# An RWKV-6 block on one core: where the first norm's statistics are computed

## The chip, the cores and the metric

The kernel runs on one core of one Trainium2 chip. The core has a matrix engine (TensorE, PE in the profile, with its weight loads shown apart as PEld), three engines for elementwise work (VectorE or DVE, ScalarE or ACT, GpSimd or POOL), and queues from which transfers are started (here those of SyncE, called SP, and of ScalarE). Each engine works through its own list of instructions strictly in order; an instruction that waits holds up everything behind it on its engine. The metric is the device time of one execution in microseconds (us).

## The reference

The input x has 32 sequences of 128 tokens with 512 channels, in float32. For each sequence the block does:

- a first layer norm over the 512 channels, and a token shift (the difference of each token to the one before it);
- five mixed inputs, each the normed x plus the shift times (a constant + a low-rank tanh product);
- from these a decay `w` by two exponentials, and the products `r`, `k`, `v` and a gate `g`, each a 512x512 matrix product;
- a recurrence over the 128 tokens with a 16x16 state for each of 32 heads, its output normed per head, times the gate, times `Wo`, added to x;
- a second layer norm and a second shift, a squared-ReLU feed-forward with a sigmoid factor, added to x.

The part that the change touches is the first line of this:

```python
m = jnp.mean(x, axis=-1, keepdims=True)
v = jnp.mean((x - m) ** 2, axis=-1, keepdims=True)
return (x - m) * jax.lax.rsqrt(v + EPS) * w + b
```

## The kernel before

The 32 sequences are worked in eight groups of four (`GB` = 4, `NG` = 8); a sequence of a group is called a block b here, with 128 tokens in the partitions and 512 channels in a row. Each group passes through streams, written as Python generators: `front_mix` (load x, first norm, shift, mixed inputs), `front_proj` (decay, k, r, v, sent by DMA to a layout with one head in each partition), `front_gate`, `prep` (what the recurrence needs besides: products of r and k, called the bonus, and decays of pairs of tokens), the recurrence in 34 units of a group (`rec_act`, `rec_state`, `rec_pool`, `rec_dve`, `rec_pe`, `rec_out`), and `back` (head norm, gate, `Wo`, second norm, feed-forward). The last group's `back` is cut in two halves, "last1" and "last2".

The order of the work is not written by hand. While the kernel is built, a planner (`Plan`, lines 73 to 179) asks every stream for its next operation, computes from its own price list when each could start, and among those that could start within `EPSILON` of the earliest takes the one with the lowest due value. The due values run, for each stream, between the two numbers of `DUE` (line 49), in units of groups. So the planner's choice fixes the order of instructions on each engine, and the chip keeps that order whatever the real times are. Buffers are part of it: an operation that needs a new tile of a kind (`alloc`) can only be taken when one of that kind is free. There are four `blk` tiles (512 columns, used to evict products on their way to DMA, for the gate, and in the bonus), two `stats`, two `mv`, two `x`, three `mx`, one `ev`, and four `ps` banks for TensorE's results.

The first norm is in `layernorm_T` (line 326), called by `front_mix` with `sums` equal to None (line 458). Its statistics are lines 333 to 342: for each of the four blocks one `bn_stats` (L339) and one `bn_aggr` (L340) on DVE, which give mean and variance in `mv`. Then, for the whole group, DVE computes variance + eps (L357), POOL raises it to the power -0.5 (L359), DVE makes -mean times that (L361), and ACT applies both to each block (L368; in the first group DVE takes every second block, L365). The normed blocks are transposed by PE (L394), and evicted by ACT and DVE.

The second norm, called by `back` with `sums` given, goes another way: the sums come for free with the addition of the residual (L884, with an accumulator), DVE turns them into minus the mean (L347), and ACT squares x minus the mean of each block with an accumulator (L354), its main output going to an `ev` tile that is overwritten later.

In the recurrence each unit needs on POOL a product (L730) and a sum of pairs (L734), on ACT two copies (L705, L716), on DVE a scan (L752) and a product (L754), and on PE eight small transposing matmuls (L787). The bonus on DVE is L660 to L680.

Of the kernel before, what the change touches and what calls it, by code (L numbers as in the profile page):

```python
# [10 lines left out]
AF = mybir.ActivationFunctionType  # L11
ALU = mybir.AluOpType
# [3 lines left out]
B, L, E = 32, 128, 512  # L16
# [19 lines left out]
PE, DVE, ACT, POOL, SP = range(5)  # L36
# [6 lines left out]
LANDING = 2.0  # L43
HOP = (0.2, 0.05, 0.05, 0.04, 0.08)
ON_POOL = (2, 3, 4)
EPSILON = 0.039


DUE = {"rec": (0.171, 0.811), "mix": (-4.351, -2.486), "proj": (-6.56, 7.24), "gate": (0.525, 0.545), "prep": (-4.001, 1.375), "back": (-0.209, 3.178), "last1": (-27.722, 1.84), "last2": (7.448, 22.404)}


class Buf:
# [20 lines left out]
class Plan:  # L73
# [103 lines left out]
    def pick(self, best):  # L177
        t0 = min(t for t, _ in best)
        return min((x for x in best if x[0] <= t0 + EPSILON), key=lambda x: x[1][3] + x[1][4] * x[1][2])


@with_exitstack
def rwkv6_block(ctx: ExitStack, tc: tile.TileContext, x, prev, s0, vecs, u, maa_w1, maa_w2,
# [11 lines left out]
    nc = tc.nc  # L195
# [76 lines left out]
    def col(v, e):  # L272
        return vec[:, v, e : e + 1]

    def bt(ap):
        return ap.rearrange("p (b t) -> p b t", t=L)
# [45 lines left out]
    def part(us, bs):  # L322

        return us if len(bs) == GB else us * len(bs) / GB + 0.03

    def layernorm_T(g, src, sums, vw, vb, which, use, take, need=None, bs=range(GB)):

        b0, nb_ = bs[0], len(bs)
        bsl, cols = slice(b0, b0 + nb_), slice(b0 * L, (b0 + nb_) * L)
        if sums is None:
            xh = src
            stats, mv = yield Op(DVE, 0.88, r=[(src, b0)], w=[(0, b0), (1, b0)], alloc=["stats", "mv"])
            for b in bs:
                if b != b0:
                    yield Op(DVE, 0.88, r=[(src, b)], w=[(stats, b), (mv, b)])
                nc.vector.bn_stats(stats[:, b, :], src[:, b, :])  # L339
                nc.vector.bn_aggr(mv[:, b, :], stats[:, b, :])  # L340
            stats.open = False
            mean, var, scale = mv[:, bsl, 0], mv[:, bsl, 1], 1.0
        else:
            mv = sums
            yield Op(DVE, 0.16, r=[(mv, b) for b in bs], w=[(mv, "m")])
            mean, var, scale = mv[:, bsl, 0], mv[:, bsl, 1], 1.0 / E
            nc.vector.tensor_scalar(mean, mean, -1.0 / E, None, ALU.mult)  # L347
            xh = None
            for b in bs:
                if xh is None:  # L350
                    (xh,) = yield Op(ACT, 0.83, r=[(src, b), (mv, "m")], w=[(0, b), (mv, ("v", b))], alloc=["ev"])
                else:
                    yield Op(ACT, 0.83, r=[(src, b), (mv, "m")], w=[(xh, b), (mv, ("v", b))])
                nc.scalar.activation(xh[:, b, :], src[:, b, :], AF.Square, bias=mv[:, b, 0:1],  # L354
                                     accum_out=mv[:, b, 1:2])
        (rstd,) = yield Op(DVE, 0.16, r=[(mv, None)], w=[(0, None)], alloc=["rstd"], port=True)
        nc.vector.tensor_scalar(rstd[:, bsl], var, scale, EPS, ALU.mult, ALU.add)  # L357
        yield Op(POOL, 1.1, r=[(rstd, None)], w=[(rstd, None)], port=True)
        nc.gpsimd.tensor_tensor(rstd[:, bsl], rstd[:, bsl], mhalf[:, bsl], ALU.pow)  # L359
        (nb,) = yield Op(DVE, 0.16, r=[(mv, None), (rstd, None)], w=[(0, None)], alloc=["nb"], port=True, end=[mv])  # L360
        nc.vector.scalar_tensor_tensor(nb[:, bsl], mean, -1.0 if sums is None else 1.0, rstd[:, bsl], ALU.mult, ALU.mult)  # L361
        for b in bs:
            if g == 0 and sums is None and b % 2:
                yield Op(DVE, 0.5, r=[(src, b), (nb, None), (rstd, None)], w=[(xh, b)], port=True)
                nc.vector.tensor_scalar(xh[:, b, :], src[:, b, :], rstd[:, b : b + 1], nb[:, b : b + 1], ALU.mult, ALU.add)  # L365
                continue
            yield Op(ACT, 0.8, r=[(src, b), (nb, None), (rstd, None)], w=[(xh, b)])
            nc.scalar.activation(xh[:, b, :], src[:, b, :], AF.Identity, bias=nb[:, b : b + 1],  # L368
                                 scale=rstd[:, b : b + 1])
        rstd.open = nb.open = False  # L370
        (xnT,) = yield Op(ACT, 0.25, w=[(0, "p")], alloc=["xnT"], need=need)
        nc.scalar.copy(xnT[:, :, 0].rearrange("p (e b) -> p e b", b=GB)[:, :, bsl],
                       pv[:, 1 - which, :, g * GB + b0 : g * GB + b0 + nb_])
        late = []

        def evict(e, pt):
            if g == 0 and sums is None:

                yield Op(DVE, 0.69, r=[(pt, None)], w=[(xnT, e)])
                nc.vector.tensor_scalar(xnT[:, e * GB + b0 : e * GB + b0 + nb_, 1 : L + 1], bt(pt[:, cols]),  # L380
                                        col(vw, e), col(vb, e), ALU.mult, ALU.add)
            else:
                yield Op(ACT, part(0.78, bs), r=[(pt, None)], w=[(xnT, e)])
                nc.scalar.activation(xnT[:, e * GB + b0 : e * GB + b0 + nb_, 1 : L + 1], bt(pt[:, cols]), AF.Identity,
                                     bias=col(vb, e), scale=col(vw, e))
            yield from use(xnT, e, pt, tiles)

        for e in range(NE):
            if e == 0:
                pt, *tiles = yield Op(PE, 0.11 * nb_, r=[(xh, None)], w=[(0, None)], alloc=["ps", *take])  # L390
            else:
                (pt,) = yield Op(PE, 0.11 * nb_, r=[(xh, None)], w=[(0, None)], alloc=["ps"])
            for b in bs:
                nc.tensor.transpose(pt[:, b * L : (b + 1) * L], xh[:, b, e * P : (e + 1) * P], ident)  # L394
            late.append((e, pt))
            if len(late) > 1:
                yield from evict(*late.pop(0))
        xh.open = False
        yield from evict(*late.pop(0))
        return (xnT, *tiles)  # L400
# [38 lines left out]
    def front_mix(g, d):  # L439
# [8 lines left out]
        def use(xnT, e, pt, tiles):  # L448
# [7 lines left out]
            nc.vector.scalar_tensor_tensor(xin[:, e, :], sx[:, e, :], col(V_MAAX, e), pt.t, ALU.mult, ALU.add)  # L456

        xnT, sx, xin = yield from layernorm_T(g, xt, None, V_LN1W, V_LN1B, 0, use, ("sx", "mx"), need)
        d["xin"] = True
        if g == 0:  # L460
# [349 lines left out]
    def back(g, d, bs=range(GB), W=None):  # L810
# [90 lines left out]
        def receptance(xnT):  # L901
# [10 lines left out]
            return xr  # L912

        xnT, xk = yield from layernorm_T(g, x1, sums, V_LN2W, V_LN2B, 1, use, ("mx",), need, bs)
        fkt = yield from get("fk", fk)
        frt = yield from get("fr", fr)
# [56 lines left out]
    for gen, n in ((rec_dve, 2), (rec_pool, 3), (rec_act, 1), (rec_state, 1), (rec_pe, 2), (rec_out, 0.1)):  # L973
        v0, v1 = DUE["rec"]
        plan.add(gen(range(NG)), v0, NG - 1 + v1, n * NU * NG)
    for g in range(NG):
        for gen, name, n in ((front_mix, "mix", 40), (front_proj, "proj", 72), (front_gate, "gate", 17),
                             (prep, "prep", 40), (back, "back", 140)):
            v0, v1 = DUE[name]
            if name != "back" or g < NG - 1:  # L980
# [4 lines left out]
    for bs, name in (((0, 1), "last1"), ((2, 3), "last2")):  # L985
        v0, v1 = DUE[name]
        plan.add(back(NG - 1, data[-1], bs, W), NG - 1 + v0, NG - 1 + v1, 130)
# [38 lines left out]
```

## Time and profile before

| | |
|---|---|
| median of 3 runs | 1524.67 us (1521.03 to 1527.92) |
| the profiled execution, own time | 1523.82 us |
| its span, first to last instruction | 1522.0 us |
| mean granted TensorE clock | 0.963 |
| PE busy, share of the span | 1407.3 us, 92% |
| DVE busy | 1264.1 us, 83% |
| POOL busy | 1036.0 us, 68% |
| ACT busy | 652.7 us, 43% |
| first norm's statistics on DVE (L339, L340), 32 blocks | 27.2 us busy |

A line such as "L339 DVE BATCH_NORM_STATS2 stats<-x" is a group of instructions of line 339 of the kernel, on DVE, that write the tile `stats` and read `x`. In the timeline, the columns are the start, the length (from the first to the end of the last of xN instructions), engine, line and operation; in square brackets is the time that the engine sat idle before it, and whose result ended that. In the table by stretches of time, each engine's busy time stands with its number of instructions in brackets, then the granted TensorE clock, the share of the DMA engines and GB/s. Successive instructions of one engine overlap a little at their ends, so their sum can exceed the time that they take in a row.

### The profile page before, as it was taken

Reading aid. Unit: us, or ns where it says so; the run is one execution under the profiler, and the core shown is the slowest. Engines: PE = TensorE matmul, PEld = TensorE weight load, DVE = VectorE, ACT = ScalarE, POOL = GpSimd, SP = SyncE. Lnnn points to the kernel's source line nnn. Section 1 sums busy time; section 2 is a strip of 40 time slices with the busy share of each in tenths; the row PEclk is TensorE's granted clock in tenths of the full one; section 3 lists DMA queues with packets and bytes.
Section 4 is the critical chain, followed back from the end, with each engine's and each line's share of the span. In section 5 each row is a group of like instructions: output and inputs, shape, how many; then the busy total and the mean of one; then the engine's idle time right before and its main releaser. Section 6 shows DMA issues by size and latency. Waiting matters only on the chain.

```text
span 1522.0 us, 16610 instructions
## 1 busy us (share of the span) xinstructions
PE 1407.3 (92%) x5344; PEld 746.5 (49%) x5344; DVE 1264.1 (83%) x1614; ACT 652.7 (43%) x1271; POOL 1036.0 (68%) x642
## 2 busy tenths in 40 slices
PE   5897988889999999999999999999999999689778
PEld 2343454445554555445544555455544555455444
DVE  6539789888998899889988899899988898878732
ACT  3333243324743356423743366423843363344252
POOL 3225884877586959687786959687786959679500
PEclk9897899899999999999999999999999999889989
DMA  6130330424304531244304521244304421400220
GB/s 225 56 87 14 118 103 15 142 82 138 118 24 139 168 102 43 80 143 135 117 31 133 184 86 42 90 143 131 111 32 140 150 98 35 159 28 29 95 71 28
DMA packets 127879, 147.04 MB, mean 97 GB/s; under 512 B 8368, under 2 KB 77616, under 8 KB 126768
## 3 DMA queue, kind: packets, MB, share of 16 engines
q1 hardware_dynamic: 91312, 127.59, 25.4%
q10 hardware_dynamic: 36480, 18.39, 4.2%
q8 instruction: 42, 0.69, 0.2%
q14 instruction: 45, 0.37, 0.1%
HBM read 94.57 MB, written 17.83 MB: 74 GB/s over the span
## 4 chain that ended last, share of the span: by engine, by line
PE 51%; DVE 21%; POOL 18%; issue 5%; ACT 3%; DMA 2%; SPq 0%; POOLq 0%; DVEq 0%; ACTq 0%
PE ps L408 18%; POOL am L730 10%; PE acc L787 8%; PE ps L965 6%; POOL a L734 6%; PE ps L949 6%; PE ps L427 5%; DVE sc L752 4%; DVE rm L754 3%; PE ps L875 2%; PE ps L414 2%; PE ps L465 2%; DVE rk L668 1%; DVE ps L660 1%; POOL mx L488 1%
## 5 line engine op out<-in xcount | busy, mean ns | idle before, releaser
L730 POOL TENSOR_TENSOR am<-v,k 128x1024 f32<-128x1024 f32 x256 | 609.0, 2379 | 34.2 <-DMA r<-blk 15.6
L408 PE MATMUL ps<-mx,wt 128*128 128x512 f32 (+1 forms) x1312 | 585.0, 593 | 17.8 <-DVE mx L456 6.6
L734 POOL TENSOR_TENSOR a<-am 128x504 f32<-128x504 f32 x256 | 286.5, 1119 | 209.4 <-DVE sc L752 183.2
L408 PEld LDWEIGHTS ps<-mx,wt 128*128 128x128 f32 x1312 | 243.8, 194 | 287.4 <-issue 261.9
L752 DVE TENSOR_TENSOR_SCAN sc<-sc,a 128x512 f32<-128x512 f32 x256 | 313.4, 1224 | 35.4 <-POOL a L734 32.3
L754 DVE TENSOR_TENSOR rm<-sc,r 128x1024 f32<-128x1024 f32 x256 | 312.8, 1222 | 32.3 <-PE acc L787 17.1
L787 PE MATMUL acc<-by_head,rm 128*128 128x128 f32 x2176 | 291.5, 284 | 39.1 <-DVE rm L754 37.0
L787 PEld LDWEIGHTS acc<-by_head,rm 128*128 128x128 f32 x2176 | 254.0, 146 | 135.8 <-DVE rm L754 53.8
L705 ACT COPY sc<-w 128x512 f32<-128x512 f32 x256 | 151.2, 591 | 250.6 <-DVE rm L754 225.7
L488 POOL TENSOR_TENSOR mx<-mx,xnT 128x512 f32<-128x512 f32 x94 | 111.6, 1198 | 72.9 <-DVE mx L486 68.7
L716 ACT COPY a<-st 128x8 f32<-128x8 f32 x256 | 51.4, 203 | 153.4 <-DVE sc L752 131.9
L949 PE MATMUL ps<-wt,mx 128*128 128x512 f32 x256 | 115.7, 594 | 0.1
L875 PE MATMUL ps<-wt,mx 128*128 128x512 f32 x256 | 113.3, 600 | 0.2 <-DVE rk L668 0.2
L965 PE MATMUL ps<-wt,ev 128*128 128x512 f32 x224 | 103.2, 604 | 2.7 <-DVE mx L493 2.7
L562 ACT COPY blk<-ps 128x512 f32<-128x512 f32 x96 | 56.0, 583 | 103.8 <-PE ps L408 94.8
L359 POOL TENSOR_TENSOR rstd<-rstd,mhalf 128x4 f32<-128x4 f32 (+1 forms) x17 | 20.2, 1191 | 116.7 <-DVE rstd L357 116.7
L486 DVE SCALAR_TENSOR_TENSOR mx<-ps,vec,sx 128x512 f32<-128x512 f32 x94 | 69.0, 743 | 25.3 <-PE ps L427 25.1
L427 PE MATMUL ps<-tha,w2p 64*128 64x512 f32 x256 | 82.2, 674 | 3.4 <-DVE mx L493 3.4
L875 PEld LDWEIGHTS ps<-wt,mx 128*128 128x128 f32 x256 | 49.1, 194 | 60.9 <-issue 56.4
L491 DVE SCALAR_TENSOR_TENSOR ps<-ps,vec,sx 128x512 f32<-128x512 f32 x66 | 49.6, 752 | 31.7 <-PE ps L427 31.3
L949 PEld LDWEIGHTS ps<-wt,mx 128*128 128x128 f32 x256 | 46.4, 190 | 51.1 <-issue 46.9
L965 PEld LDWEIGHTS ps<-wt,ev 128*128 128x128 f32 x224 | 41.1, 193 | 45.8 <-issue 40.2
(110 smaller groups left out, 1331.4 us busy)
## 6 DMA issues: line engine op xcount, KB each, us to landing
x<-in_x SPq DMA_DIRECT2D x13, 1024.0 KB
wt<-in_wk SPq DMA_DIRECT2D x8, 1024.0 KB
wt<-in_wr SPq DMA_DIRECT2D x8, 1024.0 KB
wt<-in_wg SPq DMA_DIRECT2D x8, 1024.0 KB
dgate<-blk SPq DMA_DIRECT2D x32, 256.0 KB
wt<-in_wo SPq DMA_DIRECT2D x8, 1024.0 KB
wt<-in_fk SPq DMA_DIRECT2D x8, 1024.0 KB
wt<-in_fr SPq DMA_DIRECT2D x8, 1024.0 KB
```

The lines of the kernel that those rows point to most:

```text
L408: nc.tensor.matmul(p, lhsT=w[:, c, e * P : (e + 1) * P], rhs=xin[:, c, cols], start=(c == 0), stop=(c == NE - 1))
L427: nc.tensor.matmul(p.t, lhsT=w[h, :], rhs=t[h, :], start=True, stop=True)
L488: nc.gpsimd.tensor_tensor(bt(x5[:, f, :]), bt(x5[:, f, :]), row(xnT, f, 1), ALU.add)
L705: nc.scalar.copy(sc.t, d["w01"][:, q : q + 1, :].to_broadcast([P, DH, T2]))
L730: nc.gpsimd.tensor_tensor(am.t, v[:, ds, :], k[:, q : q + 1, :].to_broadcast([P, DH, L]), ALU.mult)
L734: nc.gpsimd.tensor_tensor(a[:, :, 1:T2], am2[:, :, 0 : T2 - 1, 0], am2[:, :, 0 : T2 - 1, 1], ALU.add)
L752: nc.vector.tensor_tensor_scan(scf, scf, a.t.rearrange("p d n -> p (d n)"), 0.0, ALU.mult, ALU.add)
L754: nc.vector.tensor_tensor(pair(rm.t), sc.t.unsqueeze(3).to_broadcast([P, DH, T2, 2]), r2[:, q : q + 1, :, :].to_broadcast([P, DH, T2, 2]), ...
L787: nc.tensor.matmul(acc[:, i, :], lhsT=rm[:, i, :], rhs=by_head, is_transpose=True, start=(q == 0 and i % 4 == 0), stop=(q == S), skip_grou ...
L875: nc.tensor.matmul(p.t, lhsT=att[:, c, b * L : (b + 1) * L], rhs=wot[:, c, :], start=(c == 0), stop=(c == NE - 1))
L949: nc.tensor.matmul(p.t, lhsT=xr[:, c, b * L : (b + 1) * L], rhs=frt[:, c, :], start=(c == 0), stop=(c == NE - 1))
L965: nc.tensor.matmul(p2.t, lhsT=kv[:, c, b * L : (b + 1) * L], rhs=fvt[:, c, :], start=(c == 0), stop=(c == NE - 1))
```

## The change

For all groups but the first, the statistics of the first norm move to ACT. For each block ACT runs over x once with `Identity` and an accumulator (the sum), DVE turns the four sums into minus the mean, and ACT runs over x a second time with `Square`, minus the mean as bias, and an accumulator (the sum of squared differences). The main outputs of the eight passes go to one `blk` tile that nobody reads. The operation after it divides by 512 as the second norm's does, and since the mean is now stored with its sign turned, L361's factor changes. The first group keeps `bn_stats`. The planner's price for each pass is 0.9 us. `EPSILON` and all the due values differ too, so the order of instructions is planned anew for the whole kernel.

```diff
-EPSILON = 0.039
-DUE = {"rec": (0.171, 0.811), "mix": (-4.351, -2.486), "proj": (-6.56, 7.24), "gate": (0.525, 0.545), "prep": (-4.001, 1.375), "back": (-0.209, 3.178), "last1": (-27.722, 1.84), "last2": (7.448, 22.404)}
+EPSILON = 0.0784
+DUE = {"rec": (0.026, 0.93), "mix": (-3.979, -2.846), "proj": (-9.769, 14.248), "gate": (-1.553, 1.011), "prep": (-5.411, 0.831), "back": (-0.15, 3.099), "last1": (-40.499, -0.352), "last2": (-7.951, 22.323)}
@@ layernorm_T
-        if sums is None:
+        if sums is None and g > 0:
+
+            xh = None
+            for b in bs:
+                if xh is None:
+                    xh, mv = yield Op(ACT, 0.9, r=[(src, b)], w=[(0, b), (1, b)], alloc=["blk", "mv"])
+                else:
+                    yield Op(ACT, 0.9, r=[(src, b)], w=[(xh, b), (mv, b)])
+                nc.scalar.activation(xh.t, src[:, b, :], AF.Identity, accum_out=mv[:, b, 0:1])
+            mean, var, scale = mv[:, bsl, 0], mv[:, bsl, 1], 1.0 / E
+            yield Op(DVE, 0.16, r=[(mv, b) for b in bs], w=[(mv, "m")])
+            nc.vector.tensor_scalar(mean, mean, -1.0 / E, None, ALU.mult)
+            for b in bs:
+                yield Op(ACT, 0.9, r=[(src, b), (mv, "m")], w=[(xh, b), (mv, ("v", b))], end=[xh] if b == bs[-1] else [])
+                nc.scalar.activation(xh.t, src[:, b, :], AF.Square, bias=mv[:, b, 0:1], accum_out=mv[:, b, 1:2])
+            xh = src
+        elif sums is None:
             xh = src
             stats, mv = yield Op(DVE, 0.88, r=[(src, b0)], w=[(0, b0), (1, b0)], alloc=["stats", "mv"])
...
-        nc.vector.scalar_tensor_tensor(nb[:, bsl], mean, -1.0 if sums is None else 1.0, rstd[:, bsl], ALU.mult, ALU.mult)
+        nc.vector.scalar_tensor_tensor(nb[:, bsl], mean, -1.0 if sums is None and g == 0 else 1.0, rstd[:, bsl], ALU.mult, ALU.mult)
```

## The prediction

> **What bounds the kernel now.** I read first the busy time of each engine in stretches of the span, cut at the steady period. Four full periods, the start and the end show the shape:
>
> ```profile
> 0.00:360.00 360.00, 307.60 (x1051) 151.41 (x1052) 267.95 (x342) 123.22 (x238) 218.68 (x151) 0.91 0.32 102
> ...
> 590.00:761.00 171.00, 168.34 (x671) 89.17 (x670) 156.69 (x199) 81.10 (x159) 130.22 (x79) 1.00 0.33 106
> 761.00:931.00 170.00, 167.50 (x663) 88.33 (x662) 155.81 (x197) 80.28 (x157) 129.57 (x79) 1.00 0.33 107
> ...
> 1280.00:1437.00 157.00, 129.91 (x531) 79.55 (x529) 129.52 (x138) 58.24 (x118) 124.80 (x74) 0.90 0.17 59
> 1437.00:1522.00 85.00, 64.30 (x192) 35.66 (x192) 29.46 (x74) 33.69 (x69) 1.40 (x2) 0.90 0.23 78
> ```
>
> The first busy column is PE, the third DVE, the fourth ACT. In the middle PE is busy 167.5 of 170 us: a group costs its matmuls, and nothing else can make the period shorter than that. PE's idle time lies in the first 360 us (52 us) and after 1280 us (27 and 21 us). So DVE work that is taken away is worth only the waits of PE that it ends. The waits in the middle, 420 to 1280 us, are these, with total, count and longest:
>
> ```profile
> PE ps L394 <- DVE mx L898: 6.4, 4, 1.7
> PE ps L965 <- DVE mx L493: 2.7, 5, 0.6
> PE ps L408 <- DVE mx L910: 1.5, 4, 0.4
> PE acc L787 <- DVE rm L754: 1.1, 2, 0.7
> ```
>
> All of PE's waits for DVE there are 11.9 us with a last one of 0.2; that is the ceiling of what the middle can give. Third, the timeline of one period around the statistics, DVE, then ACT, then PE:
>
> ```profile
> 709.03 1.12 DVE L668 SCALAR_TENSOR_TENSOR rk<-ps,u_sb,rk 128x128 f32<-128x128 f32 x3
> 710.07 0.68 DVE L339 BATCH_NORM_STATS2 stats<-x 128x6 f32<-128x512 f32 x1
> ...
> 713.39 0.17 DVE L357 TENSOR_SCALAR rstd<-mv 128x4 f32<-128x4 f32 x1
> ...
> 715.34 0.68 DVE L884 SCALAR_TENSOR_TENSOR x<-ps,x 128x512 f32<-128x512 f32 x1
> ```
>
> ```profile
> 704.16 1.63 ACTq L437 DMA_DIRECT2D v<-blk  x2
> 715.13 2.93 ACT L368 ACTIVATE x<-x,nb,rstd 128x512 f32<-128x512 f32 x4 [11.00 <-DVE nb L361]
> 717.97 0.71 ACT L354 ACTIVATE ev<-x,mv 128x512 f32<-128x512 f32 x1
> ```
>
> ```profile
> 733.30 1.25 PE L394 MATMUL ps<-ident,ev 128*128 128x128 f32 x8 [1.71 <-DVE mx L898]
> ```
>
> DVE spends 3.3 us (710.07 to 713.39) on four blocks, inside a stretch in which it never rests, while ACT sits idle for 11.0 us with the norm's result as the next thing in its queue. The DVE stretch ends in L898, for which PE waits 1.71 us. That is one link from the removed work to PE. Last, the chain that ended last, in order of time, goes through the statistics in one place, in the start:
>
> ```profile
> 22.21 5.77 DMA x<-in_x
> ...
> 32.82 0.61 DVE stats L339
> 33.45 0.18 DVE mv L340
> 33.64 0.59 DVE stats L339
> 34.25 0.18 DVE mv L340
> 34.43 0.65 DVE ps L491
> ```
>
> **What is removed and added.** Removed from DVE: 28 of the 32 blocks at a pitch of 0.80 us (710.07, 710.89, 711.68, 712.48), so 22.4 us. Added to DVE: seven small operations of L347's kind, 0.17 us each, 1.2 us. Added to ACT: 28 `Square` passes at the pitch of L354 (0.71 us: 717.97, 718.67, 719.38, 720.09, the accumulator's read of 0.19 us mostly inside it), 19.9 us, and 28 `Identity` passes that the trace has not in this form; the copies of L705 (0.59 us) and L354's 0.71 us bound them, and I take 0.71, which has the accumulator. ACT gains 36.4 to 39.8 us over 652.7 and stays under 46% busy. ACT's table is loaded once in the trace and `Identity` and `Square` are both in use already, so no load is added. No DMA is added or taken away.
>
> The Trainium skill ("ScalarE: Activation LUTs", Rules for kernel authors) speaks against the move: adds and multiplies belong on VectorE rather than ScalarE. By engine time the rows agree, 1.42 us of ACT for 0.80 us of DVE. By that rule alone the sum would be 28 times 0.62, a loss of 17 us; no PE wait in the middle names ACT, so I do not charge it.
>
> **On the path, middle.** Five norms (groups 3 to 7) fall in the period's DVE stretch. The chain there is: x lands (the DMA engines fall to 0.05 busy in the stretch 708 to 709 us, so I take 709.0); four `Identity`, to 711.8; the new DVE operation, 0.17 us and at most the 1.1 us of the L668 run before it, to about 712.5; four `Square`, to 715.4; L357, POOL's L359 and L361 (0.17, 1.02, 0.15 us and handovers), to about 717. So the first norm's own result comes 2 us later than the 715.1 of now; its first transpose is at 748 us, so 30 us cover that. What counts is the second norm beside it, whose `Square` passes end at 720.79 now and lead to L898. With DVE 3.2 us ahead, its sums are complete at 713 instead of 716. If its four passes (2.8 us) go right after the first norm's, they end at 718.2, 2.6 us earlier, and the wait of 1.6 us before L394 goes (1.74, 1.60, 1.71, 1.56, 1.56 in the five periods: 8.2 us). If the first norm's L368 (2.9 us) goes first, at 717, they end at 722.8, 2 us later, and the wait grows to 3.6: a loss of 10 us. Bounds for the middle: -8.2 and +10. I take -4, half of the gain: removing this wait leaves those of L965 and L408, and which order was planned can't be read from the trace. The added wait, DVE's operation for the mean, has the bonus and L884 behind it on DVE, and behind L884 PE's banks; the planner prices a pass at 0.9 us and the row says 0.71, so the sums should be there when DVE comes to it. POOL's L359 may wait longer; the units behind it wait for DVE's scan until 727 anyway (DVE is in the bonus); if that cover were gone, 2 us in each period would fall on the recurrence.
>
> The `blk` tile: one of four is held for 6 us in each period. ACT evicts v into `blk` at 703.55 and next at 720.79, so for 17 us no eviction competes. I cost it at nothing; without that cover an eviction is late by up to 6 us.
>
> **On the path, start.** Groups 1 and 2 do their statistics at 28.0 to 34.4 us. DVE's L491 of group 0 starts at 34.35 though its matmuls (L427, from 30.93, eight in 2.82 us) give the first pair at about 32; so up to 2.1 us are freed, on the chain. Against it, ACT must fit 11.3 us of passes beside group 0's tanh, exp and evictions; it is idle 8.5 us from 35.8 to 44.3 and the rest pushes L368 of group 2 (48 to 55 us) back, which nobody waits for until 90 us. If a pass for a block that has not landed stands ahead of group 0's tanh at 27.48, that is late by 0.5 us and up to four passes: +3.3. Bounds -2.1 and +3.3; I take -2.
>
> **Order and end.** The first norm is over at 1058 us; in the last 460 us nothing of the edit itself runs. There only the new due values act, on every queue: SP's loads, ACT's DMA issues, POOL's mixing. From 1190 us on 56 units of the recurrence are left (28 from 1190 to 1313, 28 from there to 1437), at 4.4 us each, and the last group's `back` of 85 us follows. Each unit more or less that is done by the time PE's front work ends moves the end by up to 4.4 us. With no row for the new order I take 0 and bound it by four units either way, 18 us.
>
> Sum: -4 - 2 + 0 = -6. From the profiled execution, 1523.82 us (span 1522.0 and 1.8 around it, 0.9 under the median shown), that gives 1517.8; I say 1518.
>
> **Rivals.** (A) the forecast, 1518, own range 1510 to 1524. (B) The new order brings the recurrence ahead by four units before the fronts run out: -6 - 18, so 1500. For it: PE idles 48 us after 1280, which is work that could have been later; `proj` ends at a due value of 14.2 instead of 7.2, so late projections give way to `back` and the recurrence. Against: PE has no slack in the middle to give. (C) Slower: in the period, the ACT queue takes the first norm's second half and L368 ahead of the second norm's passes. +10 in the middle and +3.3 in the start: 1537. It decides once the second norm's `Square` end later than 720.8 in the period's time, 1.7 us later or more being a loss on every group. For it: the planner prices the passes too high and places by due values that favour `mix` over `back`. Against: L368 waits for a POOL operation and a gap is left meanwhile. (E) The recurrence falls four units behind, for the same due values, since projections that yield also deliver r and v late: +18, 1542. It decides if fewer units than now are done at 1190 us. Against: group 7's last front matmuls are over by 1250, 63 us before its recurrence starts. (D) The change does nothing for PE: the waits stay as they are, filled by other DVE work, 1524.
>
> On which engine to look at, the Trainium skill ("Perfetto Trace Analysis", Identifying the Most-Contended Engine) says to work on the most contended one first. PE's 167.5 of 170 us makes that PE, not DVE; by the rule the change is worth nothing, as in D, while the waits above leave at most 11.9 us in the middle.
>
> **How the numbers follow.** About 0.5%, 7.6 us, is what a measurement of this kernel can tell from no change: 1517 and 1532 are the limits. A 0.32, B 0.17, C 0.24, E 0.17, D 0.10. Faster: B's 0.17 and 0.14 of A, 0.31. Same: 0.18 of A, D's 0.10 and 0.01 of C, 0.29. Slower: the rest of C and E, 0.40. The range leaves out the outer parts of B and E, 0.15 together: 1499 to 1546. A's own is 1510 to 1524.
>
> **What would show it.** Right: L339 with 4 instructions; ACT's waits of 11.0 us before L368 replaced by passes at 0.7 us; PE's wait for L898 gone from the middle and a period of 169 us instead of 170.4 (in the chain the first L949 of a group starts at 761.12, the next at 931.50); L491 first at 32 to 33 us. Wrong: PE idle over 3 us in a period, a new wait of DVE for the mean, or fewer than 16 units between 1102 and 1190. What I can't see is the order in which the planner lays out the whole kernel; that, far more than the moved passes, would make this wrong.

## The result and the profile after

The changed kernel takes 1591.36 us (median of 4 runs, 1589.2 to 1595.34) against 1523.54 us of the kernel before (1521.03 to 1527.92): ratio 1.0442, 95% interval 1.0416 to 1.0467. The forecast of 1518 us was wrong in sign, and the time lies far above the stated range of 1499 to 1546 us. The profiled execution took 1589.2 us; its span is 1587.4 us, 65.4 more than before, at a mean granted clock of 0.946 (0.963 before).

Line numbers after the statistics are those of before plus 16: L394 is now L410, L754 is L770, L787 is L803, L898 is L914, L949 is L965. The passes are L341 (`Identity`) and L347 (`Square`), with the mean's operation at L344 between them.

First, the table by stretches of time of the kernel after. The second and the third line each run from one group's first L965 (a product in `back`) to the next group's, so each is exactly one period.

```profile
0.00:420.00 420.00, 358.18 (x1237) 178.87 (x1238) 313.11 (x397) 172.79 (x344) 251.62 (x169) 0.89 0.32 99
618.41:801.64 183.23, 173.08 (x666) 91.68 (x665) 153.83 (x191) 86.53 (x172) 126.16 (x79) 0.97 0.30 99
801.64:985.51 183.87, 173.57 (x667) 91.78 (x665) 153.81 (x191) 86.54 (x172) 126.19 (x79) 0.97 0.30 98
```

The period of before cut the same way:

```profile
760.96:931.34 170.38, 167.88 (x667) 88.71 (x665) 156.15 (x198) 80.66 (x158) 129.95 (x79) 1.00 0.33 106
```

The same 667 matmuls now take a period of 183.87 us instead of 170.38. Of the 13.5 us, 7.8 are PE standing still (10.3 us instead of 2.5) and 5.7 are PE busy longer, at a granted clock of 0.97 instead of 1.00. The start of the first L965 of each group (L949 in the kernel before) shows where the whole loss lies:

| first L949 / L965 of a group, us | group 0 | 1 | 2 | 3 | 4 | whole span |
|---|---|---|---|---|---|---|
| before | 420.01 | 590.42 | 760.96 | 931.34 | 1101.72 | 1522.0 |
| after | 436.22 | 618.41 | 801.64 | 985.51 | 1166.02 | 1587.4 |
| later by | 16.2 | 28.0 | 40.7 | 54.2 | 64.3 | 65.4 |

So 16 us are lost before the first group's `back`, 48 in the four periods after it, and 1 in all the rest, as the difference of 4.8 us more up to group 5's first L965 (1337.97 us, 1268.84 before) and 3.8 us won back after it.

What PE waits for in the period from 801 to 985 us (total, times, longest):

```profile
PE acc L803 <- DVE rm L770: 4.2, 3, 1.7
PE ps L410 <- DVE mx L914: 3.4, 2, 2.0
PE ps L981 <- DVE mx L502: 0.8, 1, 0.8
PE ps L443 <- DVE mx L502: 0.8, 1, 0.8
PE ps L965 <- DVE mx L502: 0.8, 1, 0.8
```

That is 10.0 of the 10.3 us, all of it for DVE, which has less to do than before (153.8 us in a period, 156.2 before). The wait for L914, which the change was forecast to end, has grown to 3.4 us, and those for the recurrence (L770) are new in the period. Those for the mixing are 2.4 us (L502), where 0.5 us stood before (L965 for L493). DVE's own waits show where its time goes. From 430 to 1100 us, after:

```profile
DVE ps L970 <- PE ps L981: 23.5, 11, 4.4
DVE sc L768 <- POOL a L750: 19.0, 20, 2.0
DVE mx L502 <- PE ps L443: 16.0, 16, 2.1
DVE mx L914 <- ACT ps L911: 10.4, 12, 1.8
```

and in the same stretch of the kernel before, where L954, L752 and L486 are the first three of these:

```profile
DVE mx L486 <- PE ps L427: 12.7, 8, 2.2
DVE sc L752 <- POOL a L734: 11.9, 22, 1.0
...
DVE ps L954 <- PE ps L965: 0.9, 4, 0.2
```

DVE stands 23.5 us before L970, the end of a group's feed-forward, where it stood 0.9. PE's timeline at that place shows both engines waiting for each other in turn:

```profile
834.98 1.12 PE L443 MATMUL ps<-tha,w2p 64*128 64x512 f32 x2 [0.84 <-DVE mx L502]
836.95 5.40 PE L981 MATMUL ps<-wt,ev 128*128 128x512 f32 x8 [0.84 <-DVE mx L502]
```

```profile
842.45 0.70 DVE L970 SCALAR_TENSOR_TENSOR ps<-th,ps 128x512 f32<-128x512 f32 x1 [4.42 <-PE ps L981]
```

The mixing of one group (L443 on PE, L502 on DVE) and the end of another group's `back` (L981 on PE, L970 on DVE) are now cut into each other. L981 can't start until L502 has freed a bank, and DVE then has L970, which needs all eight matmuls of L981, as the next thing in its queue: it stands 4.42 us. The eight matmuls take 5.40 us, at a granted clock of 0.68 from 836.95 to 842.30 us; eight such ones take 3.60 elsewhere.

### The profile page after: what moved, and what is told of

Its sections match the earlier page's. It is cut to its first block, busy times and chain, and to the rows that moved or that the text cites. A ratio compares the mean times of both kernels' runs of the same rounds, so it can differ in the third digit from the quotient of the medians.

```text
span 1587.4 us, 16643 instructions
## 1 busy us (share of the span) xinstructions
PE 1430.2 (90%) x5344; PEld 759.5 (48%) x5344; DVE 1253.8 (79%) x1565; ACT 694.3 (44%) x1383; POOL 1022.8 (64%) x642
## 4 chain that ended last, share of the span: by engine, by line
PE 58%; DVE 20%; POOL 10%; issue 5%; ACT 4%; DMA 2%; SPq 0%; ACTq 0%; POOLq 0%; DVEq 0%
PE ps L424 21%; PE acc L803 9%; PE ps L981 6%; POOL am L746 6%; PE ps L891 6%; PE ps L965 6%; PE ps L443 6%; DVE sc L768 4%; DVE rm L770 3%; POOL a L750 3%; DVE mx L502 2%; PE ps L430 2%; PE ps L481 2%; PE ps L410 1%; POOL mx L504 1%
## 5 line engine op out<-in xcount | busy, mean ns | idle before, releaser
L424 PE MATMUL ps<-mx,wt 128*128 128x512 f32 (+1 forms) x1312 | 592.5, 600 | 6.7 <-DVE mx L914 1.4
L750 POOL TENSOR_TENSOR a<-am 128x504 f32<-128x504 f32 x256 | 269.4, 1052 | 226.1 <-DVE sc L768 204.3
L424 PEld LDWEIGHTS ps<-mx,wt 128*128 128x128 f32 x1312 | 247.0, 197 | 278.9 <-issue 245.6
L803 PE MATMUL acc<-by_head,rm 128*128 128x128 f32 x2176 | 294.1, 285 | 66.8 <-DVE rm L770 59.2
L803 PEld LDWEIGHTS acc<-by_head,rm 128*128 128x128 f32 x2176 | 254.6, 146 | 173.8 <-DVE rm L770 93.8
L770 DVE TENSOR_TENSOR rm<-sc,r 128x1024 f32<-128x1024 f32 x256 | 312.7, 1221 | 30.5 <-PE acc L803 16.7
L504 POOL TENSOR_TENSOR mx<-mx,xnT 128x512 f32<-128x512 f32 x94 | 115.0, 1235 | 126.8 <-DVE mx L502 122.5
L965 PE MATMUL ps<-wt,mx 128*128 128x512 f32 x256 | 115.8, 595 | 4.2 <-DVE mx L502 4.2
L981 PE MATMUL ps<-wt,ev 128*128 128x512 f32 x224 | 105.1, 614 | 3.4 <-DVE mx L502 3.4
L443 PE MATMUL ps<-tha,w2p 64*128 64x512 f32 x256 | 91.7, 690 | 12.7 <-DVE mx L502 5.9
L375 POOL TENSOR_TENSOR rstd<-rstd,mhalf 128x4 f32<-128x4 f32 (+1 forms) x17 | 16.7, 981 | 127.0 <-DVE rstd L373 127.0
L502 DVE SCALAR_TENSOR_TENSOR mx<-ps,vec,sx 128x512 f32<-128x512 f32 x94 | 68.1, 742 | 31.9 <-PE ps L443 31.8
L965 PEld LDWEIGHTS ps<-wt,mx 128*128 128x128 f32 x256 | 46.3, 190 | 56.1 <-issue 46.9
L981 PEld LDWEIGHTS ps<-wt,ev 128*128 128x128 f32 x224 | 42.4, 198 | 52.2 <-issue 45.0
```

The source lines that it names most:

```text
L424: nc.tensor.matmul(p, lhsT=w[:, c, e * P : (e + 1) * P], rhs=xin[:, c, cols], start=(c == 0), stop=(c == NE - 1))
L443: nc.tensor.matmul(p.t, lhsT=w[h, :], rhs=t[h, :], start=True, stop=True)
L504: nc.gpsimd.tensor_tensor(bt(x5[:, f, :]), bt(x5[:, f, :]), row(xnT, f, 1), ALU.add)
L750: nc.gpsimd.tensor_tensor(a[:, :, 1:T2], am2[:, :, 0 : T2 - 1, 0], am2[:, :, 0 : T2 - 1, 1], ALU.add)
L770: nc.vector.tensor_tensor(pair(rm.t), sc.t.unsqueeze(3).to_broadcast([P, DH, T2, 2]), r2[:, q : q + 1, :, :].to_broadcast([P, DH, T2, 2]), ...
L803: nc.tensor.matmul(acc[:, i, :], lhsT=rm[:, i, :], rhs=by_head, is_transpose=True, start=(q == 0 and i % 4 == 0), stop=(q == S), skip_grou ...
```

## The experiments

All kernels with "old order" or "new order" take a list in place of the planner's choice. While before and after were planned, the stream taken at each step was written down; the kernel then takes streams in that order, and prices, `EPSILON` and due values no longer matter:

```diff
-            best = []
...
-            t, st = self.pick(best)
+            key = ORDER[0][ORDER[1][n]]
+            n += 1
+            (st,) = [x for x in self.streams if x[5] == key]
+            t = self.start(st[1])
+            assert t is not None, key
```

Where the edit has more operations than the list has places, the surplus goes at the place of the fourth block's statistics; where it has fewer, places are dropped. Places are counted in the recorded list, which has 5402 of them for the kernel before. Each of these kernels has its own line numbers, so its rows are best followed by operation and tile.

**Edit and order apart.** The first run has the edit of `layernorm_T` with the list of before, the second has `bn_stats` on DVE with the list of after.

> The edit alone, in the order of the kernel before: the planner's choices are replaced by the recorded list of the kernel before, and the nine operations of the new statistics stand where the four of the old ones stood (the mean and the four Square passes right after the fourth Identity). Theory 1, the order: the moved passes cost little, the new due values laid out a worse order. Then this is near the kernel before, 1515 to 1545 us, with a period of 169 to 174 us. Theory 2, the edit: ACT's passes hold up ACT, DVE waits for the sums and the second norm comes late in every period. Then this is near the changed kernel, 1570 to 1595 us, with a period of 180 us or more.

> The order alone: bn_stats on DVE as before, all else in the recorded order of the changed kernel (the old operations stand where the four Identity passes stood). Theory 1, the order: 1575 to 1610 us, with PE waits of some 10 us in each period. Theory 2, the edit: 1515 to 1545 us, since the passes on ACT are gone.

Measured: 1541.35 us (1.0115, 1.010 to 1.013) and 1606.39 us (1.0542, 1.0525 to 1.0558). With the two kernels this makes a square:

| us | `bn_stats` on DVE | edit |
|---|---|---|
| order of before | 1524 | 1541 |
| order of after | 1606 | 1591 |

The new order costs 82 us without the edit and 50 with it. The edit costs 17 us in the old order and gains 15 in the new one. So the loss is the order's, and the edit by itself is a smaller loss, of 1.15%, in the order that the kernel had.

**Values and code.** The edit with `EPSILON` and `DUE` of before, and the code of before with those of after, both planned anew.

```diff
-EPSILON = 0.0784
-DUE = {"rec": (0.026, 0.93), "mix": (-3.979, -2.846), "proj": (-9.769, 14.248), ...
+EPSILON = 0.039
+DUE = {"rec": (0.171, 0.811), "mix": (-4.351, -2.486), "proj": (-6.56, 7.24), ...
```

> The edit with the old due values and the old EPSILON, planned anew. If the new values as such are bad (theory 1a), this is near the kernel before, 1515 to 1545 us. If it is that any list of due values fits one list of operations only (theory 1b), the planner goes astray with the old values too, and this is slower than before by more than 2%, above 1555 us, perhaps slower than the changed kernel. Theory 2, the edit: as the changed kernel, 1570 to 1600 us.

> The old statistics on DVE with the new due values and the new EPSILON, planned anew. Theory 1a, the new values are bad for any list of operations: 1575 to 1610 us. Theory 1b, they fit the changed list only: slower than the changed kernel, above 1595 us. Theory 2, the edit: near the kernel before, 1515 to 1545 us.

Measured: 1637.74 us (1.0751, 1.0732 to 1.077) and 1606.28 us (1.0537, 1.0515 to 1.0559). The new values are slow with either list of operations, 1591 and 1606 us. The old ones are the best with one and the worst with the other: the values that give 1524 us with one list of operations give 1638 us with a list in which 28 of 5402 have given way to 63. So what a set of values is worth depends on the list of operations that it orders.

**The mean's way over DVE.** Why does the edit cost 17 us in the old order? The timelines of DVE and POOL in that run, around the statistics of one group:

```profile
717.88 2.25 DVE L358 TENSOR_SCALAR mv<-mv 128x4 f32<-128x4 f32 x1
723.55 0.17 DVE L387 TENSOR_SCALAR rstd<-mv 128x4 f32<-128x4 f32 x1 [3.42 <-ACT blk L361]
```

```profile
717.76 2.34 POOL L760 TENSOR_TENSOR am<-v,k 128x1024 f32<-128x1024 f32 x1
```

L358 turns four sums per partition into means. It takes 2.25 us instead of the 0.17 of the same operation in the second norm, and ends with POOL's product at 720.1. ACT's `Square` passes wait for it, and DVE then stands 3.42 us before L387 for them. The end of the second norm is queued behind, and so PE's wait for L928 (L898 of before) rises to 2.55 us. Two runs leave the operation out. The accumulator gives minus the mean by itself, in both orders:

```diff
-                nc.scalar.activation(xh.t, src[:, b, :], AF.Identity, accum_out=mv[:, b, 0:1])
+                nc.scalar.activation(xh.t, src[:, b, :], AF.Identity, scale=-1.0 / E, accum_out=mv[:, b, 0:1])
...
-            yield Op(DVE, 0.16, r=[(mv, b) for b in bs], w=[(mv, "m")])
-            nc.vector.tensor_scalar(mean, mean, -1.0 / E, None, ALU.mult)
```

> As the first run (the edit in the order of the kernel before, 1541 us), but the mean never goes to DVE: Identity gets a scale of -1/512, so that ACT's accumulator is minus the mean itself, and the eight passes follow each other. In that run DVE's operation for the mean took 2.25 us instead of 0.17, as long as POOL's product L760 ran beside it, and ACT then had waited 2.70 us. Theory: this hold and the round trip over DVE are what the edit costs in the old order, 2 to 3 us in each of five periods: 1526 to 1532 us. Rival: the cost is that DVE waits in order for ACT's Square passes (3.4 us before L387 in each period); the round trip only moves that wait: 1535 to 1542.

> The changed kernel in its own order with the same change: no operation for the mean on DVE, all else where it stood. There the mean took 1.54 us in each period and ACT waited 5.2 us for it. If the round trip is what makes the changed kernel slow: 1545 to 1565 us. If the laid-out order is, with its waits of PE for L770, L502 and L914: 1580 to 1592.

Measured: 1526.11 us (1.0014, 1.0002 to 1.0026) in the old order and 1587.79 us (1.0424, 1.0402 to 1.0446) in the new one. In the old order 15 of the 17 us were this one operation and its waits. In the new order it is worth 3.6 us by the medians, and the intervals of the two kernels overlap.

**What DVE's statistics are worth.** The first run keeps the order of before and leaves the statistics of groups 1 to 7 out, the second does each `bn_stats` of these groups twice.

```diff
+                if g > 0:
+                    nc.vector.memset(mv[:, b, :], 1.0)
+                    continue
                 nc.vector.bn_stats(stats[:, b, :], src[:, b, :])
```

```diff
                 nc.vector.bn_stats(stats[:, b, :], src[:, b, :])
+                if g > 0:
+                    nc.vector.bn_stats(stats[:, b, :], src[:, b, :])
```

> The kernel before in its own order with bn_stats and bn_aggr of groups 1 to 7 left out (a tiny memset of the mean and variance stands in each place, so the norm of these groups is not computed): DVE is freed of 0.7 us per block and ACT has nothing added. This is the gain that the prediction counted on, by itself. Prediction's step: the wait of 1.6 us before L394 goes in five periods and 2 us in the start: 1512 to 1517 us. Rival: other work of DVE or PE's matmuls take its place, and nothing is gained: 1521 to 1526.

> The kernel before in its own order with bn_stats of groups 1 to 7 done twice: 0.66 us more of DVE per block, 2.6 us per norm, at the place in question. If the DVE stretch between the statistics and L898 is on PE's path, each period grows by 2.6 us or more (the wait before L394, and a lower clock after a longer wait), and the start by up to 5: 1540 to 1556 us. If DVE has slack there: 1524 to 1530.

Measured: 1517.0 us (0.9954, 0.9937 to 0.997) and 1543.69 us (1.0127, 1.0104 to 1.0151). Leaving this work out altogether, in this order, gave 8 us. Adding 0.66 us for each of 28 blocks, 18.5 us of DVE, costs 19 us. By group, the run without statistics has its first L949 3.6 us earlier in group 0 (416.41) and 5.6 in group 4 (1096.14): 3.6 us of the gain are made in the start, and 0.5 us in a period, which stays at 169.9 us, of which PE is busy 167.9. The run has a cost of its own: in groups 4 to 7 DVE's operation before the power, 0.17 us in the kernel before (713.39 us), now meets POOL's product and takes 2.10 us:

```profile
706.16 2.10 DVE L374 TENSOR_SCALAR rstd<-mv 128x4 f32<-128x4 f32 x1
```

```profile
705.88 2.35 POOL L747 TENSOR_TENSOR am<-v,k 128x1024 f32<-128x1024 f32 x1
```

So its 8 us are not the price of 22 us of DVE alone. The most that the four middle periods could give is the time that PE idles in them, 2.5 us each.

**The wait before rstd.** In the run without the mean, DVE still stood before rstd:

```profile
714.49 0.17 DVE L385 TENSOR_SCALAR rstd<-mv 128x4 f32<-128x4 f32 x1 [2.93 <-ACT blk L359]
```

In the next run rstd, the power and the bias of groups 3 to 7 stand 14 places later in the list and their apply passes 25 places later, and the eight passes of every group all stand where the first block's statistics were.

> The statistics by two ScalarE passes without the mean's operation on VectorE, in the recorded order of the kernel before, with one change to that order: for groups 3 and later the three operations that turn the sums into rstd and bias are placed 14 picks later and the four apply passes 25 picks later. In the run without that shift (1526.11 us) VectorE stood 2.93 us before rstd, waiting for the last Square pass. Theory (VectorE's wait before rstd is what eats the gain that the freed VectorE time should give): 1518 to 1523 us, the wait before rstd gone. Rival (the freed time has no further worth, and a later apply only delays the transposes of the next group): 1525 to 1530 us.

Measured: 1526.07 us (1.0022, 1.0008 to 1.0036). The wait is gone (L385 at 715.03 stands behind other work) and the time is the same. The theory was wrong: DVE's wait in the middle hid nothing, since the period was 170.4 us with it and without. That is also the period of the kernel before, though DVE has no statistics to do here and L385 takes 0.16 us (DVE is busy 154.1 us in a period, 156.2 before): PE still idles 2.2 us in it, 1.1 of them for L926 (L898 of before). What remains lies in the start. In this run:

```profile
34.44 0.17 DVE L385 TENSOR_SCALAR rstd<-mv 128x4 f32<-128x4 f32 x1 [9.06 <-ACT blk L359]
```

```profile
34.94 7.48 PE L455 MATMUL ps<-tha,w2p 64*128 64x512 f32 x16 [4.67 <-ACT tha L497]
```

Group 1's eight passes stand in ACT's queue ahead of group 0's tanh (L497), and rstd in DVE's queue ahead of group 0's mixing.

**The order without the work.** The list of after, and no statistics for groups 1 to 7.

> The order of the changed kernel, with the first norm's statistics of groups 1 to 7 left out altogether (the place of mean and variance is filled by a memset, so the norm isn't computed for those groups). It carries neither VectorE's statistics nor ScalarE's passes. Theory 1 (the new order is slow because the statistics' work sits in the wrong places of it): well below 1588 us, 1570 or less. Theory 2 (the order of everything else, the projections against the output stages and the recurrence, is what costs): 1575 to 1592 us, that is at least 50 us over the kernel before although it does less work.

Measured: 1583.23 us (1.0399, 1.038 to 1.0419), 66 us above the same work in the old order. The period is 181.7 us (mean of four), and PE's waits in one of them are those of after, though neither DVE nor ACT has any statistics to do:

```profile
PE acc L804 <- DVE rm L771: 3.5, 3, 1.4
PE ps L411 <- DVE mx L915: 3.4, 2, 2.0
PE ps L982 <- DVE mx L503: 0.8, 1, 0.8
PE ps L444 <- DVE mx L503: 0.8, 1, 0.8
PE ps L966 <- DVE mx L503: 0.8, 1, 0.8
```

DVE's wait for the end of `back` is the same 23.5 us too:

```profile
DVE ps L971 <- PE ps L982: 23.5, 11, 4.4
```

So it is the order of all the rest, not where the statistics lie in it. That the handing to and fro between mixing and `back` is the costly part of it is read from these waits; no run changed that alone.

**The start.** Two runs test what the start is worth. The first is the edit without the mean, shifted as above, with the passes of groups 1 and 2 placed behind group 0's mixing:

```diff
 group 1, places in the list
-  eight passes 52, rstd 60, apply from 67
+  eight passes 143 to 151, rstd 157, apply from 167
 group 2
-  eight passes 63, rstd 93, apply from 107
+  eight passes 222 to 229, rstd 237, apply from 250
```

> The run before this one of the same kind (statistics by two ScalarE passes, no operation of VectorE for the mean, order of the kernel before with a later second half for groups 3 to 7) took 1526.07 us. Its period in the middle is the 170.4 us of before, but group 0's k projection starts at 56.9 us instead of 55.0, since group 1's eight passes stand in ScalarE's queue ahead of group 0's tanh, and VectorE waits 9.1 us for them with group 0's mixing queued behind. Here the passes of groups 1 and 2 are placed behind group 0's mixing: group 1's beside its k projection, group 2's beside its r projection. Theory (the freed VectorE time is worth something in the start alone, as in the run without statistics, whose first middle group starts 3.6 us earlier than in the kernel before): the k projection starts at 49 to 51 us, the total is 1518 to 1522 us, a little under the kernel before. Rival (the start is bound by the arrival of weights and by the recurrence, so that an earlier k projection only waits later): 1523 to 1527 us.

Measured: 1522.27 us (0.9991, 0.9979 to 1.0003), not told from before. The k projection does start at 50.85 us, and the total is 4 us under the run without this move. The second has nothing of the edit: the kernel before, `bn_stats` on DVE, with the list of before and the statistics of groups 1 and 2 moved in it:

```diff
 group 1, places in the list
-  bn_stats 52 to 58, rstd 60, apply from 67
+  bn_stats 133, rstd 133, apply from 145
 group 2
-  bn_stats 63 to 88, rstd 93, apply from 107
+  bn_stats 183, rstd 183, apply from 250
```

> Nothing of the edit: all statistics stay on VectorE as bn_stats, in the order of the kernel before, with one change: the statistics of groups 1 and 2 are placed later, group 1's behind the mixing of group 0 (VectorE rests 13.8 us beside the k projection), group 2's in front of the mixing of group 1 (VectorE rests 10.4 us), and their rstd, bias and apply passes behind them. Theory 1 (the few us that the start gives belong to the place of the statistics in the order, not to the engine that does them): the k projection starts at 49 to 51 us instead of 55, the middle is as before, 1517 to 1521.5 us. Theory 2 (the gain of the run before, 1522.27 us, needs VectorE to be freed): 1522 to 1526 us.

Measured: 1518.48 us (0.9976, 0.9965 to 0.9987), 0.24% under the kernel before, a small difference whose interval doesn't reach 1. PE and DVE in its start:

```profile
51.20 9.27 PE L422 MATMUL ps<-mx,wt 128*128 128x512 f32 x17
```

```profile
49.72 0.68 DVE L353 BATCH_NORM_STATS2 stats<-x 128x6 f32<-128x512 f32 x1
...
67.99 0.76 DVE L505 SCALAR_TENSOR_TENSOR ps<-ps,vec,sx 128x512 f32<-128x512 f32 x1 [12.37 <-PE ps L441]
```

The k projection starts at 51.2 us instead of 55.0, and DVE does group 1's statistics at 49.7 us, behind group 0's mixing and inside a stretch in which it still rests 12.37 us afterwards. The first L949 of group 0 comes at 416.36 us and that of group 4 at 1098.09, both 3.6 us earlier than before, and the middle is unchanged. At group 0 that is all that leaving the statistics out gave (416.41). So what was had in the start belongs to the place of the statistics, and needs no other engine.

## Why the prediction was wrong

**The step that failed: "Order and end".** It took 0 for the new order, bounded it by 18 us either way, four units of the recurrence, and said that "only the new due values act" in the last 460 us. The runs give +50 us with the edit and +82 without it, and +66 with no statistics on either side. The size was wrong and so was the place: of the 65 us, 64 are lost before 1166 us, where the prediction let only the edit act, and 1 after it, in the part for which the bound was taken. "PE has no slack in the middle to give" was used against a gain there; it says just as well that a new order of the whole list can only lose there. The bound should have come from the period: PE idles only 2.5 us of 170.4 in it, so a different list has almost nothing to gain there and as much to lose as waits can grow, once in each period. The closing sentence does name the order, which "far more than the moved passes, would make this wrong"; but no term of the sum and no bound priced it in the middle. What makes the new order cost so much in a period is the interleaving of mixing and `back` as far as the waits show, and that part of the cause stays open.

**Middle, -4.** The price of the freed DVE time was of the right kind but too large: with no statistics at all, and rstd held four times, the four middle periods give 2 us; with the statistics on ACT, no operation for the mean and rstd not held, they give nothing (170.4 us). The link "statistics, DVE stretch, L898, PE" is real, as 18.5 us more on DVE cost 19 us; it doesn't run as far the other way: PE's matmuls fill 167.9 us of the period. The edit was not this saving, however. The cost of the mean's operation, "0.17 us and at most the 1.1 us" of the run before it, was 2.25 us in the old order and 1.54 in the new one, and the sentence that the sums "should be there when DVE comes to it" put the wait on the wrong side: in the old order the sums were there, the mean was held, and then ACT waited for the mean and DVE for ACT. That made 15 of the 17 us. The bound of +10 for the middle came nearest: from group 0's first L949 to group 4's the edit in the old order lost 12.1 us.

The passes were also priced a little low. In after, from the timeline of ACT:

```profile
915.18 0.63 ACT L341 ACTIVATE blk<-x 128x512 f32<-128x512 f32 x1 [1.25 <-DMA x<-in_x]
...
924.55 0.72 ACT L347 ACTIVATE blk<-x,mv 128x512 f32<-128x512 f32 x1 [5.16 <-DVE mv L344]
```

They start every 0.75 and 0.85 us, not every 0.71, which adds 5 us to ACT over the kernel. Between the two kinds ACT stands 5.16 us, which the prediction had as 0.7: the mean's operation starts only at 922.97 us, behind other work in DVE's queue, and is held for 1.4 us more. Little of this lies on PE's path in this order, since leaving the operation out gave 3.6 us in all.

**Start, -2.** The condition of its upper bound, "a pass for a block that has not landed stands ahead of group 0's tanh", is what happened. The chain of after goes through the passes there:

```profile
22.01 5.95 DMA x<-in_x
27.98 0.73 ACT blk L341 x2
28.73 0.73 ACT blk L341 x2
29.46 0.02 issue
29.48 0.72 ACT blk L341 x2
30.20 0.48 ACT tha L485
```

The first tanh is at 30.11 us instead of 27.48. That is the smaller part of the 16.2 us by which group 0's first L965 is late: in the new order without any statistics it is 9.7 us late already (429.66), so most of the loss in the start is the order's too. In the old order the edit comes to group 0's first L949 4.7 us late, and 0.9 us late without the mean's operation. The gain that the same step hoped for can be had, 3.6 us instead of 2.1, by moving the statistics within DVE's queue.

**The rivals.** C had the sign, the mechanism of a later second norm, and 1537 us; the edit in the old order took 1541. In that run, where L398 applies the first norm and L384 is the second norm's first pass:

```profile
725.50 2.93 ACT L398 ACTIVATE x<-x,nb,rstd 128x512 f32<-128x512 f32 x4 [1.50 <-DVE nb L391]
728.33 0.71 ACT L384 ACTIVATE ev<-x,mv 128x512 f32<-128x512 f32 x1
```

```profile
726.22 0.17 DVE L377 TENSOR_SCALAR mv<-mv 128x4 f32<-128x4 f32 x1
```

The second norm's mean is ready at 726.39 us, and its passes stand behind the first norm's in ACT's queue until 728.33, as C had it. They stood so in the kernel before too (L368 and L354, 715.13 and 717.97); what is new is that the first norm's are late, because of its mean and of DVE's wait after it. E foresaw that the order would lose, by the recurrence falling behind. At 1190 us 191 of its units are begun, 200 before, so E's sign is there; but 88.3 us after group 4's first L965 or L949 they are 201 and 200. The recurrence is late with all the rest and not behind it, and the end costs 1 us. No rival had the order losing in every period. B and D fell.

**What would show it.** L339's successor with four instructions was seen, and ACT's gap filled with passes, though with 5.16 us left between the two kinds. PE's wait for L898 did not go, it grew from 1.6 to 3.4 us in a period, and the period is 183.9 us and not 169. "PE idle over 3 us in a period" and "a new wait of DVE for the mean" had been named as signs of a wrong forecast, and both are there, the second as a wait of ACT for the mean.

## What to carry to other kernels

When a list schedule is fitted to its operations, a changed list must be judged apart from its new schedule: replay the old order with the edit and the new order without it, before believing either. An operation that goes to another engine and back for a number costs the queues on both sides, not its own time (15 us in the old order for seven operations of 0.17 us), so let the accumulator's scale give the number if it can. And before moving work to an idle engine, look whether the same work can stand elsewhere in its own engine's queue: here that gave 0.24%, where the best form of the move (1522.27 us) could not be told from no change.

## What the runs showed of the hardware

**A small DVE operation is held by POOL's product.** In after, the mean's operation and the product on POOL end together at 924.5 us:

```profile
922.97 1.54 DVE L344 TENSOR_SCALAR mv<-mv 128x4 f32<-128x4 f32 x1
```

```profile
921.80 2.69 POOL L746 TENSOR_TENSOR am<-v,k 128x1024 f32<-128x1024 f32 x1
```

Over the seven groups the operation takes 0.17 us at the least and 1.54 in the median, 2.08 in the median in the old order. In both kernels those that start while a product or a sum of POOL runs end within 0.04 us of its end, and the others take 0.17 us. The Trainium skill ("SBUF — State Buffer", Who interferes with whom) says that a `tensor_scalar` on DVE can take the port pair that it shares with GpSimd, and that the second to issue blocks until the first is done. These rows agree: POOL's instruction starts first, and DVE's ends with it, as rstd's does in the run without statistics (2.10 us). The planner has a mark, `port=True`, that keeps such operations apart from POOL's; rstd and the bias carry it, the new operation for the mean does not.

**The granted clock falls after short waits.** In after, from PE's timeline:

```profile
945.66 0.66 PE L410 MATMUL ps<-ident,ev 128*128 128x128 f32 x4 [2.00 <-DVE mx L914]
947.76 1.11 PE L410 MATMUL ps<-ident,ev 128*128 128x128 f32 x4 [1.44 <-DVE mx L914]
948.67 6.13 PE L424 MATMUL ps<-mx,wt 128*128 128x512 f32 x8
```

In the edit with the old order, and in the kernel before (after the wait of 1.71 us that the prediction shows):

```profile
743.27 1.25 PE L424 MATMUL ps<-ident,ev 128*128 128x128 f32 x8 [2.55 <-DVE mx L928]
745.87 4.64 PE L438 MATMUL ps<-mx,wt 128*128 128x512 f32 x8
```

```profile
735.27 3.60 PE L408 MATMUL ps<-mx,wt 128*128 128x512 f32 x8
```

Waits of 2.00 and 1.44 us with 0.66 us of work between them are followed by eight matmuls in 6.13 us instead of 3.60, at a granted clock of 0.50 from 948.00 to 952.80 us. One wait of 2.55 us is followed by eight in 4.64 us (0.53 from 744.40 to 748.00); a wait of 1.71 us by eight in 3.60 (1.00 from 735.27 to 738.70). So a wait that grew from 1.7 to 2.55 us cost clock as well, and so did shorter ones close together: in a period of after PE's matmuls take 5.7 us longer, beside the 7.8 us of standing. The Trainium skill ("TensorE: Matmul & The Clock Gate", Part 1, What's actually happening) has the clock fall after an idle window of about 3.4 us; here no single wait is that long, and the lower clock is seen all the same; the rows decide.

**DVE beside a full PE is worth more in one direction.** 18.5 us more on DVE cost 19 us, while 22 us less gave 8, about half of it in the start and with rstd held four times, and with the statistics on ACT the period stayed at 170.4 us.
